# Three branch results summed by accumulating transfers from GpSimd's queue instead of VectorE additions, in a deformable-convolution kernel

## The chip, the cores and the metric

The kernel runs on one core of a Trainium2 chip. The metric is the time of one execution on the device in microseconds, the median over runs. The engines are called as in the profile: PE (TensorE, matmuls), PEld (its weight loads), DVE (VectorE), ACT (ScalarE), POOL (GpSimd) and SP (SyncE, which here only issues transfers). A trailing q, as in SPq, is an engine's own instruction queue.

## The reference, cut to what matters

Two layers act on x of 2 images x 256 channels x 128 x 128 pixels, float32. The change lies in the first one. Three branches with dilations 1, 9 and 12 each sample the image at learned offsets, weigh nine taps, normalise over the channels of each pixel and apply Gelu. Their results and a 1x1 convolution are added; normalisation, a two-layer network per pixel and another normalisation follow.

```python
def _branch(x, w_off, w_def, lw, lb, pad, dil):
    off = _conv(x, w_off, pad, dil)                  # 18 offsets per pixel
    y = _deform_dw(x, off, w_def, pad, dil)          # nine bilinear samples, weighed
    return gelu(_ln2d(y, lw, lb))                    # over the 256 channels of a pixel
...
x1 = _branch(x, off_w1, def_w1, bw1, bb1, 1, 1)
x2 = _branch(x, off_w2, def_w2, bw2, bb2, 9, 9)
x3 = _branch(x, off_w3, def_w3, bw3, bb3, 12, 12)
c = einsum('bchw,oc->bohw', x, conv_w[:, :, 0, 0]) + conv_b
out = _ln2d(x1 + x2 + x3 + c, n1_w, n1_b)
h = gelu(out @ mlp_w1.T + mlp_b1) @ mlp_w2.T + mlp_b2     # per pixel
out = _ln2d(h + out, n2_w, n2_b)
```

In the whole, x + layer0(groupnorm(x)) goes into a second layer of the same form, a 3x3 convolution with ternary weights.

## The kernel before, in words

There are three stages. The first, to about 916 us, takes the group norm's moments, writes a padded pixel-major copy of x to memory (`tables`), computes the offsets, and writes for every branch, tap and row the weights of the bilinear samples (`hats`). The second, the branch stage, runs from 916 to about 5840 us. The third, to the end, is the second layer.

The branch stage (`sample_near`) works in units: image, pair of rows, branch; 2 x 66 x 3 = 396 units. For each unit and each half of the channels, `sample` multiplies eleven tiles `xs` of the table (loaded at L1326) by a matrix `A` (matmul L1468 into `pm`), ACT copies the result to `ev` (L1480), and `accumulate` adds the taps into a ring of rows in SBUF (`ring`, DVE L1429, with a first touch by ACT at L1411). `A` for a unit is the product of the two tiles `hy` and `hx` (DVE L1367), which `load_hats` fetches from `hats` (L1347, three buffers of each) as soon as the product three items earlier has freed one.

Whenever four rows of one branch are finished (a group: 64 groups of 4 rows x 128 pixels over both images), a chain of further steps begins: the generator `PixelTail.branch`. It turns the group to pixel-major form `v` of 128 partitions x 1024 values (transposes L905 and L913, ACT copy L921), takes moments (DVE L1101 to L1106), the power -1/2 on POOL (L1107, L1108), then ACT applies scale, bias and Gelu (`scaled`, L1115). The three branches of a group finish at different times, as their dilations differ, so that the sum goes through memory: branch 0 stores `v` to `g12d` (L1179), branch 1 loads that into the tile `other` (L1186), adds (L1189) and stores the sum (L1191), and branch 2 loads the sum (L1186), adds (L1198) and goes on with it. It loads `xn`, adds the 1x1 convolution (matmul and DVE addition of `product`, L1137 and L1145), normalises, transposes back to `S` (L1154, L1221), computes the network (`hp` L890 into `hT`, `h2` L1137), normalises again and stores `x1d` (L1260).

All engine orders are the program's own: work is recorded in the order in which the Python code runs, and `pin` keeps it. The chains are interleaved with the sampling by hand. `sample` calls `tail.advance()` twice for each unit and half of the channels; each call is one step, in which every chain whose time has come runs to its next `yield`. A `yield` gives up to three values: the steps to wait, the number of buffers that the chain claims from then on, and a flag by which only one flagged chain runs per step. Nine buffers (`VBUFS`) of one rotation hold `v`, `other`, `xn`, `S`, `hT` and `xr`, and `may` lets a chain run only if the claims fit. The set `stored` tells which branch's transfer to `g12d` has been issued; branches 1 and 2 of a group wait for their predecessor there. When sampling is over, the remaining chains run step by step alone; this drain takes from about 5700 to 5840 us.

All plain transfers in this stage are issued by SP, in order. SP stops at a transfer whose source is not ready, and what is behind it stops with it.

Of the kernel before, what the change touches and what calls it, by code (L numbers as in the profile page):

```python
# [14 lines left out]
ALU = mybir.AluOpType  # L15
# [56 lines left out]
def conv_preact_kernel(ctx: ExitStack, tc: tile.TileContext, t: dict, out: bass.AP):  # L72
    nc = tc.nc
# [634 lines left out]
    with ExitStack() as actx:  # L708
        psum = actx.enter_context(tc.tile_pool(name="ps_a", bufs=1, space=PSUM))

        def gps():
# [4 lines left out]
        k = {  # L716
            "dxs": dxs,
            "zero": ap.tile([P, C], F32, name="zero"),
            "wz": ap.tile([P, KC, NZ], F32, name="wz"),
            "shift": ap.tile([P, len(dxs), P], F32, name="shift"),  # L720
            "mid": ap.tile([P, ZG, NOFF], F32, name="mid"),
            "hatw": ap.tile([P, 2, NTAP * NH], BF16, name="hatw"),
            "parts": [ap.tile([P, 2, ZG, P], BF16, name=f"parts{i}") for i in range(3)],
            "zr": ap.tile([P, ZRING, NZ], F32, name="zr"),
# [110 lines left out]
    class Tail:  # L835
# [135 lines left out]
        def branch(self, b, br, g, y):  # L971

            pin = self.pin
            cols = slice(g * NG, (g + 1) * NG)
            gv = g12d[b].rearrange("(k p) f -> p k f", p=P)[:, :, cols]
            z = []
            yield from self.normalised(z, y, (b, br, g))
            v = z[0]
            for c in range(KC):
                pin(  # L980
                    nc.scalar.activation(
                        v[:, c, :], z[1 + c], AF.Gelu,
                        scale=bw[:, br, c : c + 1], bias=bb[:, br, c : c + 1],
                    )
                )
            if br == 0:
                yield 2
                nc.sync.dma_start(gv, v)
                self.stored.add((b, br, g))
                return  # L990
            yield 1, 1 + br
            other = self.tile("other")
            while (b, br - 1, g) not in self.stored:
                yield 1
            nc.sync.dma_start(other, gv)
            if br == 1:
                yield 2
                pin(nc.vector.tensor_tensor(v, v, other, ALU.add))
                yield 2
                nc.sync.dma_start(gv, v)  # L1000
                self.stored.add((b, br, g))
                return
            xn = self.tile("xn")
            nc.sync.dma_start(xn, x[b].rearrange("(k p) h w -> p k (h w)", p=P)[:, :, cols])
            yield 4
            for c in range(KC):
                pin(
                    nc.scalar.activation(
                        xn[:, c, :], xn[:, c, :], AF.Identity, bias=negmean[b][:, c : c + 1]
                    )  # L1010
                )
            yield 1
            yield from self.finish(b, g, v, other, xn)
# [75 lines left out]
    class PixelTail(Tail):  # L1089
# [70 lines left out]
        def branch(self, b, br, g, y):  # L1160

            pin = self.pin
            gv = g12d[b].rearrange("c f -> (c f)").rearrange("(g p e) -> g p e", p=P, e=KC * NG)[g]
            xv = x[b].rearrange("(k p) h w -> p k (h w)", p=P)[:, :, g * NG : (g + 1) * NG]
            yield from self.entered()
            yield 0, 1, True
            v = self.tile("v")
            vf = v.rearrange("p k n -> p (k n)")
            vv = vf.rearrange("p (j c) -> p j c", c=C)
            rows = [vv[:, j, :] for j in range(NG // P)]  # L1170
            self.turned(vv, y, (b, br, g))
            self.read.add((b, br, g))
            rs = self.moments(rows)
            yield 7, min(1 + br, 2), True
            yield from self.scaled(rows, rs, AF.Gelu)
            self.norms -= 1
            if br == 0:
                yield 2
                nc.sync.dma_start(gv, vf)  # L1179
                self.stored.add((b, br, g))  # L1180
                return
            other = self.tile("other")
            of = other.rearrange("p k n -> p (k n)")
            while (b, br - 1, g) not in self.stored:
                yield 1
            nc.sync.dma_start(of, gv)  # L1186
            if br == 1:
                yield 2
                pin(nc.vector.tensor_tensor(vf, vf, of, ALU.add))  # L1189
                yield 2  # L1190
                nc.sync.dma_start(gv, vf)  # L1191
                self.stored.add((b, br, g))
                return
            yield 1, 3
            xn = self.tile("xn")
            nc.sync.dma_start(xn, xv)
            yield 2
            pin(nc.vector.tensor_tensor(vf, vf, of, ALU.add))  # L1198
            yield 2, 2, True
            for c in range(KC):  # L1200
                pin(
                    nc.scalar.activation(  # L1202
                        xn[:, c, :], xn[:, c, :], AF.Identity, bias=negmean[b][:, c : c + 1]
                    )
                )
            yield 1
            pairs = [(xn[:, c, :], convs[b][:, c, :]) for c in range(KC)]
            adds = [self.product("pc1", vv, convb3, pairs, h) for h in range(2)]
            yield 1, 1
            for add in adds:  # L1210
                add()
            yield 2
            yield from self.entered()
            rs = self.moments(rows)
            yield 7, None, True
            yield from self.scaled(rows, rs, AF.Identity)
            self.norms -= 1
            yield 2, 2, True
            S = self.tile("S")
            for c in range(KC):  # L1220
                pin(nc.scalar.copy(S[:, c, :], self.channels(rows, c)))  # L1221
            yield 1, 3
            hT = []
            for m in range(MC):
                if m % KC == 0:
                    hT.append(self.tile("hT"))
                hp = self.bank("hp")
                self.matmul(hp, [(w1[:, c, m * P : (m + 1) * P], S[:, c, :]) for c in range(KC)])
                pin(
                    nc.scalar.activation(  # L1230
                        hT[-1][:, m % KC, :], hp, AF.Gelu, bias=b1[:, m : m + 1]
                    )
                )
                yield 1, 4 if m < MC - 1 else 3
            pairs = [(hT[m // KC][:, m % KC, :], w2[:, m, :]) for m in range(MC)]
            add = self.product("h2", vv, b23, pairs, 0)
            yield 1, 3
            add()
            add = self.product("h2", vv, b23, pairs, 1)
            yield 1, 1  # L1240
            add()
            yield 2, 2
            yield from self.entered()
            rs = self.moments(rows)
            xr = self.tile("xr")
            nc.sync.dma_start(xr, xv)
            yield 7, None, True
            yield from self.scaled(rows, rs, AF.Identity)
            self.norms -= 1
            yield 2  # L1250
            for c in range(KC):
                zc = self.channels(rows, c)
                pin(
                    nc.vector.scalar_tensor_tensor(
                        xr[:, c, :], zc, n2w[:, c : c + 1], xr[:, c, :], ALU.mult, ALU.add
                    )
                )
                pin(nc.vector.bn_stats(stats2[b][:, c, g, :], xr[:, c, :]))
            yield 2, 1
            nc.sync.dma_start(  # L1260
                x1d[b].rearrange("(k p) f -> p k f", p=P)[:, :, g * NG : (g + 1) * NG], xr
            )
# [365 lines left out]
    with cmp.Else():  # L1628
        with ExitStack() as bctx:
            psum = bctx.enter_context(tc.tile_pool(name="ps_b", bufs=1, space=PSUM))  # L1630
            pool = bctx.enter_context(tc.tile_pool(name="bpool", bufs=1))
            k = {
                "A": [pool.tile([PX, 9, RI, WA], F32, name=f"A{i}") for i in range(2)],
            }
# [356 lines left out]
```

## Time and profile before

| | |
|---|---|
| median of 3 runs | 6637.6 us (6625.94 to 6637.77) |
| the profiled execution's own time | 6632.7 us |
| its span | 6630.8 us |
| busy over the span: PE, DVE, ACT, POOL | 95%, 89%, 63%, 10% |
| TensorE clock granted, mean | 0.974 of full speed |
| moved by the DMA engines | 1360 MB, 205 GB/s on average |
| loads `other` (L1186), 512 KB | 128 |
| stores to `g12d` (L1179, L1191), 512 KB | 64 and 64 |
| additions L1189, L1198 | 64 and 64, 1.22 us each |

The profile is of one execution. A group of instructions in it gives line, engine, operation, what is written and read, shape and count, then the busy time in us and the mean of one in ns, then the engine's idle time just before them and what ended most of it. The chain is the sequence of work that ended last, followed back from the last instruction to what released each step. A busy share of PE is not a share of its peak, since matmuls are pipelined and their ends are modelled.

### The profile page before, as it was taken

To read this page: it belongs to the slowest core of one execution; us is meant where nothing else is said; L and a number is where in the kernel's file an instruction comes from. 1 tells how busy PE (TensorE), PEld (TensorE's weight loads), DVE (VectorE), ACT (ScalarE), POOL (GpSimd) and SP (SyncE) were. 2 spreads that over 40 slices of the span, in tenths; PEclk is the share of its full clock that TensorE was granted. 3 is DMA by queue.
4 is the path that set the end of the run, shared out by engine and by line. 5 is a ranking of instruction groups with operands and counts; after the bars stand their busy time and mean duration, and the time that the engine had idled before them with its cause. 6 is when DMAs were issued, how large, how long until landed. Compare 5 with 4: busy or idle time off the path is not lost.

```text
span 6630.8 us, 100591 instructions
## 1 busy us (share of the span) xinstructions
PE 6275.4 (95%) x32242; PEld 4993.0 (75%) x32242; DVE 5906.2 (89%) x13772; ACT 4189.3 (63%) x8690; POOL 686.7 (10%) x665
## 2 busy tenths in 40 slices
PE   6899978999999999999999999999999999989999
PEld 3455558888888888888888888888888888734444
DVE  8766668999999999999778999999999999689996
ACT  2344447777777777777676777777777777554442
POOL 0000000111111111111110111111111111200000
PEclk9999978999999999999999999999999999989999
DMA  8976667877787777787667877788777777343332
GB/s 290 274 214 199 201 169 216 226 217 219 223 225 217 223 217 224 222 222 206 181 194 203 227 219 219 221 223 227 223 217 220 215 222 209 122 164 132 139 139 90
DMA packets 635795, 1360.49 MB, mean 205 GB/s; under 512 B 109592, under 2 KB 290344, under 8 KB 618736
## 3 DMA queue, kind: packets, MB, share of 16 engines
q1 hardware_dynamic: 617328, 1318.97, 68.9%
q10 hardware_dynamic: 17408, 33.56, 1.6%
q8 instruction: 261, 4.28, 0.3%
q14 instruction: 286, 2.34, 0.1%
q0 software_dynamic: 512, 1.34, 0.1%
HBM read 1087.10 MB, written 266.47 MB: 204 GB/s over the span
## 4 chain that ended last, share of the span: by engine, by line
PE 53%; DVE 30%; DMA 8%; ACT 5%; issue 3%; SPq 0%; POOL 0%; DVEq 0%; ACTq 0%; POOLq 0%
PE pm L1468 22%; DVE ring L1429 13%; PE pc L1810 6%; PE hp L890 6%; PE h L1137 5%; DVE A L1367 5%; PE pz L364 4%; DMA hx<-hats 3%; PE pc L1137 3%; DMA xa<-in_x 3%; ACT ev L1480 2%; ACT v L1115 2%; DVE st L1101 1%; PE ph L463 1%; PE tp L905 1%
## 5 line engine op out<-in xcount | busy, mean ns | idle before, releaser
L1468 PE MATMUL pm<-A,xs 96*128 96x216 f32 (+2 forms) x17424 | 3248.5, 343 | 176.4 <-ACT ev L1480 45.4
L1468 PEld LDWEIGHTS pm<-A,xs 96*128 96x128 f32 x17424 | 3049.1, 195 | 374.1 <-ACT ev L1480 119.2
L1429 DVE SCALAR_TENSOR_TENSOR ring<-ev,defw,ring 128x256 f32<-128x256 f32 (+4 forms) x6372 | 2481.2, 451 | 98.1 <-ACT ev L1480 47.8
L1480 ACT COPY ev<-pm 128x432 f32<-128x432 f32 (+4 forms) x4488 | 1987.5, 483 | 869.3 <-PE pm L1468 695.8
L1367 DVE TENSOR_TENSOR A<-hy,hx 96x768 f32<-96x768 f32 (+1 forms) x1124 | 1009.5, 945 | 164.1 <-DMA hx<-hats 89.8
L1107 POOL TENSOR_TENSOR rs<-rs,mhalf 128x4 f32<-128x4 f32 x320 | 472.0, 1475 | 4202.5 <-DVE rs L1106 3543.9
L1810 PE MATMUL pc<-cring,signs 128*128 128x512 bf16 x3456 | 757.9, 382 | 17.0 <-ACT cring L1727 7.4
L1115 ACT ACTIVATE v<-v,rs 128x256 f32<-128x256 f32 x1280 | 694.4, 594 | 16.7 <-POOL rs L1108 16.6
L1810 PEld LDWEIGHTS <-signs 128*128 128x128 bf16 x3456 | 339.6, 98 | 434.6 <-issue 27.7
L890 PE MATMUL hp<-S,w 128*128 128x512 f32 x1024 | 493.9, 607 | 0.8 <-ACT S L1221 0.8
L364 PE MATMUL pz<-wz,xa 128*128 128x486 f32 x1024 | 461.6, 578 | 25.3 <-DVE zr L371 25.3
L1137 PE MATMUL h<-w,hT 128*128 128x256 f32 x2048 | 477.1, 379 | 0.0
L1101 DVE BATCH_NORM_STATS2 st<-v 128x6 f32<-128x256 f32 x1280 | 446.9, 410 | 30.8 <-ACT v L921 30.8
L1411 ACT ACTIVATE ring<-ev,defw 128x256 f32<-128x256 f32 (+1 forms) x856 | 404.5, 485 | 24.2
L1137 PEld LDWEIGHTS h<-w,hT 128*128 128x128 f32 x2048 | 369.3, 190 | 65.5 <-issue 1.0
L364 PEld LDWEIGHTS pz<-wz,xa 128*128 128x128 f32 x1024 | 189.2, 191 | 189.3 <-issue 126.1
L921 ACT COPY v<-tp 128x512 f32<-128x512 f32 x384 | 207.8, 598 | 182.7 <-PE tp L913 182.4
L1230 ACT ACTIVATE hT<-hp,b 128x512 f32<-128x512 f32 x256 | 176.1, 688 | 218.6 <-PE hp L890 214.6
L890 PEld LDWEIGHTS hp<-S,w 128*128 128x128 f32 x1024 | 196.7, 197 | 139.4 <-issue 121.3
L470 ACT ACTIVATE hb<-ph 96x512 f32<-96x512 f32 (+1 forms) x384 | 209.8, 596 | 144.2 <-PE ph L463 135.6
L1137 PE MATMUL pc<-convw,xn 128*128 128x256 f32 x1024 | 271.1, 393 | 2.4 <-ACT xn L1202 2.4
L371 ACT COPY zr<-pz 128x486 f32<-128x486 f32 x128 | 72.1, 564 | 256.5 <-PE pz L364 253.8
(246 smaller groups left out, 5132.5 us busy)
## 6 DMA issues: line engine op xcount, KB each, us to landing
hy<-hats SPq DMA_DIRECT2D x1112, 288.0 KB
hx<-hats SPq DMA_DIRECT2D x1112, 288.0 KB
xs<-tables SPq DMA_DIRECT2D x1452, 96.0 KB
g12d<-v SPq DMA_DIRECT2D x128, 512.0 KB
other<-g12d SPq DMA_DIRECT2D x128, 512.0 KB
hats<-hb SPq DMA_DIRECT2D x64, 720.0 KB
hats<-hb SPq DMA_DIRECT2D x64, 576.0 KB
xa<-in_x ACTq DMA_DIRECT2D x64, 512.0 KB
```

The source lines that it names most:

```text
L364: nc.tensor.matmul(pz[:, 0:NZ], lhsT=xt[:, c, r, :], rhs=k["wz"][:, c, :], start=c == 0, stop=c == KC - 1,)
L890: nc.tensor.matmul(out, lhsT=w, rhs=v, start=i == 0, stop=i == n - 1)
L1101: pin(nc.vector.bn_stats(st[:, j, :], rows[j]))
L1107: nc.gpsimd.tensor_tensor(rs[:, 0, :], rs[:, 0, :], mhalf[:, 0:n], ALU.pow)
L1115: nc.scalar.activation(row, row, func, scale=rs[:, 0, j : j + 1], bias=rs[:, 1, j : j + 1])
L1137: nc.tensor.matmul(bank[:, j, :], lhsT=v[:, px], rhs=w, start=False, stop=i == len(pairs) - 1,)
L1367: nc.vector.tensor_tensor(dst, hy[:, i0:i1].rearrange("p i t w -> p t i w"), hx[:, i0:i1].rearrange("p i t w -> p t i w"), ALU.mult,)
L1411: pin(nc.scalar.mul(dst, src, w))
L1429: pin(nc.vector.scalar_tensor_tensor(dst, src, w, dst, ALU.mult, ALU.add))
L1468: nc.tensor.matmul(pv[:, j, :, m0:m1, :], lhsT=xts[b, Rt][t][:, c * P : (c + 1) * P], rhs=A[:, y0:y1, m0:m1, AO + t * CI : AO + (t + 1) * CI],
L1480: nc.scalar.copy(dst.rearrange("p m (t j) -> p t m j", j=CI), pm[:, 0 : len(ts), 0:n].rearrange("p t (m j) -> p t m j", j=CI),)
L1810: nc.tensor.matmul(pc, lhsT=signs[:, k, (h * 3 + t) * 3 + kx, m * P : (m + 1) * P], rhs=xc[:, i, k, t * JC : (t + 1) * JC, kx : kx + W], s ...
```

## The change

Branch 1 no longer loads `other`, adds and stores: GpSimd issues one transfer that adds `v` onto the values in `g12d`. Branch 2 no longer loads and adds either: GpSimd issues one transfer that adds the values in `g12d` onto `v` in SBUF. The tile `other` is gone, and with it 128 loads and 64 stores of SP and 128 additions of DVE. Branch 1 and branch 2 claim one buffer instead of two while they wait for the moments. Branch 1 marks its result as stored four steps earlier. Branch 2 waits the same number of steps up to its next ACT work, one and four instead of one, two and two, and claims two buffers instead of three meanwhile.

```diff
@@ PixelTail.branch
             rs = self.moments(rows)
-            yield 7, min(1 + br, 2), True
+            yield 7, 1, True
             yield from self.scaled(rows, rs, AF.Gelu)
...
-            other = self.tile("other")
-            of = other.rearrange("p k n -> p (k n)")
             while (b, br - 1, g) not in self.stored:
                 yield 1
-            nc.sync.dma_start(of, gv)
             if br == 1:
-                yield 2
-                pin(nc.vector.tensor_tensor(vf, vf, of, ALU.add))
-                yield 2
-                nc.sync.dma_start(gv, vf)
+                nc.gpsimd.dma_start(gv, vf, accum_op=ALU.add)
                 self.stored.add((b, br, g))
                 return
-            yield 1, 3
+            nc.gpsimd.dma_start(vf, gv, accum_op=ALU.add)
+            yield 1, 2
             xn = self.tile("xn")
             nc.sync.dma_start(xn, xv)
-            yield 2
-            pin(nc.vector.tensor_tensor(vf, vf, of, ALU.add))
-            yield 2, 2, True
+            yield 4, 2, True
```

In the changed kernel the accumulating transfer of branch 1 stands at L1185, that of branch 2 at L1188; the lines up to L1179 keep their numbers, and those after the edit are seven lower (L1326, L1347, L1367, L1429, L1468 and L1480 become L1319, L1340, L1360, L1422, L1461 and L1473).

## The prediction

> **What bounds the kernel now.** I read the span by stages first. The branches run from about 916 to 5700 us; before them lies the offset stage, after them a drain to 5840 and the second layer, neither of which the change touches except the drain. The table of busy time by stage:
>
> ```profile
> core 0: us, PE busy (x) PEld busy (x) DVE busy (x) ACT busy (x) POOL busy (x), PEclk, DMA share, GB/s
> 916.00:5700.00 4784.00, 4614.24 (x24864) 4115.21 (x24865) 4451.39 (x11227) 3415.48 (x7664) 656.98 (x620) 0.98 0.77 216
> 5700.00:5840.00 140.00, 115.26 (x501) 78.92 (x500) 71.35 (x243) 64.99 (x122) 22.52 (x33) 0.90 0.29 101
> ```
>
> PE is busy 96%, DVE 93%, the DMA engines 77%, POOL 14%. PE leaves 4784 - 4614 = 170 us idle: no relief of another engine can give more in this stage, unless PE's long matmul records hide gaps (matmul ends are modelled, so some do). Two engines are nearly full, so I read the groups for what the additions cost, then the chain for how many of them lie on the path.
>
> ```profile
> L1189 DVE TENSOR_TENSOR v<-v,other 128x1024 f32<-128x1024 f32 x64 | 77.9, 1218 | 2.0 <-DMA other<-g12d 1.9 <-issue 0.2
> ...
> L1198 DVE TENSOR_TENSOR v<-v,other 128x1024 f32<-128x1024 f32 x64 | 77.7, 1214 | 0.0
> ```
>
> The two additions take 1.22 us each, and cost DVE 1.13 us from one start to the next. DVE waits for their operand 1.9 us in all: the loads are well hidden. The chain that ended last, 2215 to 2240 us (start, duration, what):
>
> ```profile
> 2214.99 2.29 DVE ring L1429 x6
> 2217.28 1.13 DVE v L1198
> 2218.42 0.41 DVE ring L1429
> 2218.82 0.14 SPq L1347
> 2218.96 0.05 issue
> 2219.01 5.46 DMA hx<-hats
> ...
> 2235.49 0.11 DVE v L1189
> 2235.60 0.09 issue
> 2235.68 0.02 DVEq L1367
> 2235.70 0.91 issue
> 2236.61 2.69 DVE A L1367 x3
> ```
>
> Both additions are on it here. The second is cut into four pieces because the chain steps to the semaphore instruction behind it, but 2235.49 to 2236.61 is all DVE inside that addition. Read in this way, 100 us at a time, the chain holds 42 of the 128 additions, 45 us together. Elsewhere the path is in PE (L1468, L890, L1137), and an addition there is cover. The path also enters hats loads, 5.46 us here.
>
> The SP queue's waits from 1300 to 5600 us (total us, times, longest):
>
> ```profile
> SPq L1347 <- DVE A L1367: 771.5, 463, 15.3
> SPq L1326 <- PE pm L1468: 680.2, 894, 14.3
> SPq L1191 <- DVE v L1189: 345.8, 54, 8.1
> SPq L1179 <- ACT v L1115: 245.7, 52, 8.4
> SPq L1347 <- DVE ring L1429: 208.3, 452, 2.1
> SPq L1186 <- PE h L1137: 140.3, 27, 6.9
> ```
>
> SP stands for 486 us (L1191, L1186) on the very steps that the change takes from it, in front of the hats loads. But most of the time the load behind would have waited for L1367 anyway.
>
> **What the Trainium skill says.** "DMA: Bandwidth & Descriptors", section on SWDGE, HWDGE and iDMA: an accumulating transfer must be issued by GpSimd, whose cores write its descriptors; the same page, "Issuing engines are not separate DMA queues": all queues end in the same 16 engines. "Collectives: The Full Stack", section on the bandwidth ceiling: an add inside a transfer is not slow by its arithmetic but by its two source reads, and ran at about half the rate of a copy. "SBUF — State Buffer", "Who interferes with whom": DVE instructions with two SBUF inputs contend with GpSimd instructions that read SBUF. The trace of before has no accumulating transfer, so it can't confirm the second and third; it agrees that POOL is uneven (L1107, the same 128x4 power, takes 1006 to 2548 ns).
>
> **The change part by part.**
>
> *DVE loses 128 additions.* On the path 45 us go. Of the other 86 (97 us) some would surface once the path moves; I take a tenth, -10. Bounds of the two together: -26 if PE takes over wherever it was just behind (26 is about what remains if only the pieces named as additions count), -100 if DVE's slack of 7% is what makes PE wait.
>
> *SP loses 128 loads of `other` (median 527 ns to issue) and 64 stores (326 ns)*: 67 + 21 = 88 us of issuing, and the 486 us of standing. SP's own pieces in the chain from 1300 to 5600 us sum to only 11 us, so I take -5; bounds 0 and -25. SP still stands at L1179.
>
> *POOL gains 128 transfers to issue.* The nearest row is the gather of 128 rows, L565, 987 ns each: 126 us on an engine with 4127 us free. Each waits in POOL's own order, for ACT's last Gelu of that `v` and, in branch 2, for the landing of branch 1's accumulation. What is queued behind is the next power L1107 and product L1108, which ACT needs in L1115. Who waits for that now:
>
> ```profile
> L1108 POOL TENSOR_TENSOR rs<-rs x320: 198/409/4867, 1040.5 to 5825.7; 128x4 f32<-128x4 f32 x160
> ...
> who waited for it (us, times):
>   ACT v L1115: 16.6, 3
> ```
>
> Three waits in 320, because the code puts 7 steps between them. A step is 4784 us / (396 units x 2 halves x 2) = 3.0 us, so some 20 us are allowed. An issue of 1 us and a few us of waiting for ACT fit: 0. Bounds 0 and +40. The wait for branch 1's landing is also covered in the steady part: in the built order its accumulation stands 88 calls of L1468 ahead, at 66 calls per 37 us some 49 us.
>
> *The data in flight.* Branch 2's accumulation into `v` has 1 + 4 + 1 + 1 = 7 steps, 21 us, before L1145 adds into the same `v`; if it lands later, DVE stops in order and everything behind with it. At the page's fit for GpSimd's path ("Anatomy of one DMA", 2 us + bytes / 436 GB/s) twice 512 KB takes 4.4 us, an estimate; the crowded hats loads show 5.5 us for 288 KB. I expect 5 to 10 us. Covered.
>
> *The DMA engines.* Per group of four rows before: one store, load, store, load = 4 copies. After: one store and two accumulations at two copies each = 5. A copy of 512 KB takes 216 GB/s / 0.77 = 281 GB/s, 1.9 us of all engines. So 64 x 1.9 = 120 us more on 77%, two and a half points. Loads make up some 6% of the chain from 1300 to 5600 (252 us: hx 172, xs 53, hy 27), so +7; bounds -10 (accumulation as cheap as a copy) and +120.
>
> *Buffers.* `other` leaves the rotation of 9, and the hold at the 7-step wait falls from 2 to 1. In the built order the stores of x1d move by a few L1468 calls only (the last inside the loop from the 8702nd to the 8698th), and both programs have 340 calls of tail matmuls after the last L1468. So the schedule stays: 0, bounds -10 and +10.
>
> *The drain, 5700 to 5840.* Here steps pass without sampling between them, so cover is thin: POOL meets L1185 and L1188 close together, waiting for landings with powers behind. Four groups finish here. I take +8, bounds -8 (seven additions gone) and +25.
>
> Sum: -45 - 10 - 5 + 7 + 8 = -45 us against the profiled execution's 6632.7, which gives 6588. The median of the runs, 6637.6, lies 4.9 above that execution, inside the runs' own spread of 12. I put the same 4.9 on top: **6593**.
>
> **The rivals.**
>
> *Accumulating transfers clog the DMA engines: slower.* If each costs three copies or more, a group takes 1 + 3 + 3 = 7 copies, DMA share rises by 64 x 3 x 1.9 / 4784 = 8 points, and hats or xs loads behind one are 3.8 us later (two extra copies). Today some 46 loads (252 / 5.5) are on the path for some 350 units, 13%; at one in five late loads on the path, 128 x 3.8 x 0.2 = +97, less the 45 + 10 + 5 of gains, plus 8: 6685. It decides from about 2.2 us of extra engine time per accumulation (128 x 2.2 x 0.2 = 56). For it: hats loads on the chain already, DMA 77% busy. Against: the page's halved rate, not a third, and the freed SP queue.
>
> *POOL stands, and the powers come late: slower or even.* The point is a stand over some 12 us less the issue. At +40 the sum is about even, 6633. Against it: POOL is 86% idle, and in steady state what its transfers wait for is long past.
>
> *PE binds at once: no change.* PE's waits there name ACT's copies of `ev`, 54.6 us, and of `S`, 41.5; only part of the first goes back to DVE. Then 45 shrinks to 15 or 20, and drain and DMA give it back: 6630. Against: the many stretches like the quoted one, in which DVE and a load alternate.
>
> *That the additions are not really replaced*: the built order has 128 accumulating transfers on POOL and no addition on DVE. Out.
>
> **How the numbers follow.** A measurement tells about 0.2%, 13 us, from no change. Forecast 0.70, its own range 6540 to 6624, all faster; PE binds 0.08, within 0.2%; DMA engines 0.17 and POOL 0.05, slower. The range takes the large end of DVE's gain (-100 with SP's -15: 6525) and the DMA rival's value: 6525 to 6688, leaving out the worst of that rival and little below.
>
> **What would show it.** Right: DVE's busy time falls by some 150 us with L1189 and L1198 gone; PE's idle time in the branch stage falls from 170 us toward 125; SP's waits at L1191 and L1186 vanish; ACT still hardly waits for L1108; L1145 does not wait for the new transfers. Wrong: DVE's wait for hx (89.8 us over the stage now) doubling, a DMA share at 85% or more, L1145 or L1108 appearing as long waits, the drain growing by over 25 us.

## The result, and the profile after

The changed kernel takes 6615.5 us (median of 12 runs) against 6636.9 before (12 runs). The ratio is 0.9968, with a 95% interval of 0.9957 to 0.9978: 21 us faster, 15 to 29. Forecast were 45: the direction is right, the size is not. The profiled execution took 6623.9 us (span 6622.0), near the upper end of the runs (6600.6 to 6627.6), so its trace is read for causes and the runs for sizes.

The changed kernel's busy time by stage, to be held against the prediction's first table:

```profile
core 0: us, PE busy (x) PEld busy (x) DVE busy (x) ACT busy (x) POOL busy (x), PEclk, DMA share, GB/s
916.00:5700.00 4784.00, 4617.54 (x24891) 4117.20 (x24892) 4327.25 (x11125) 3415.70 (x7675) 770.18 (x743) 0.98 0.78 209
5700.00:5840.00 140.00, 109.05 (x478) 74.83 (x477) 65.88 (x232) 65.85 (x118) 25.39 (x38) 0.89 0.41 120
```

In the branch stage DVE does 124 us less, and PE 3 us more. DVE was relieved as planned; PE got nearly nothing of it in this execution. So the question is what DVE does with the time. Its waits from 1300 to 5600 us (us in total, times, longest), the kernel before:

```profile
DVE A L1367 <- PE pm L1468: 66.7, 51, 4.6
DVE ring L1429 <- ACT ev L1480: 43.8, 48, 2.8
DVE A L1367 <- DMA hx<-hats: 43.5, 38, 6.1
```

and the changed one:

```profile
DVE A L1360 <- PE pm L1461: 120.3, 62, 7.3
DVE A L1360 <- DMA hx<-hats: 90.1, 89, 3.7
DVE ring L1422 <- ACT ev L1473: 49.5, 50, 3.6
```

Two waits have about doubled. The first is good news: DVE is now ahead and waits until PE has read the old `A`. The second is a loss: 89 times instead of 38, DVE stands for the weights `hx`, which are late. (Over the whole stage, 916 to 5700 us, it goes from the 89.8 us of the prediction to 133.7: not doubled, but of the signs of being wrong that the prediction named it is the one that moved.)

On SP the waits for the two steps are gone, and the same time stands at others (changed kernel, 1300 to 5600 us):

```profile
SPq L1340 <- DVE A L1360: 1017.9, 454, 15.5
SPq L1319 <- PE pm L1461: 534.7, 850, 10.1
SPq L1179 <- ACT v L1115: 403.4, 52, 11.0
SPq L1253 <- DVE xr L1247: 299.0, 51, 7.9
```

The 486 us at L1191 and L1186 are gone. Instead SP stands 246 us more at the hats loads (772 to 1018), which wait for a free buffer, 191 more at the store of `x1d` (108 to 299) and 158 more at L1179, and 145 less at the `xs` loads. Here the queue mostly changed the place where it stands.

### The profile page after: what moved, and what is told of

Its sections match the earlier page's. It is cut to its first block, busy times and chain, and to the rows that moved or that the text cites. A ratio compares the mean times of both kernels' runs of the same rounds, so it can differ in the third digit from the quotient of the medians.

```text
span 6622.0 us, 100200 instructions
## 1 busy us (share of the span) xinstructions
PE 6280.3 (95%) x32242; PEld 4993.8 (75%) x32242; DVE 5768.3 (87%) x13644; ACT 4184.2 (63%) x8690; POOL 801.1 (12%) x793
## 5 line engine op out<-in xcount | busy, mean ns | idle before, releaser
L1461 PE MATMUL pm<-A,xs 96*128 96x216 f32 (+2 forms) x17424 | 3238.6, 342 | 168.9 <-ACT S L1214 45.1
L1461 PEld LDWEIGHTS pm<-A,xs 96*128 96x128 f32 x17424 | 3045.8, 194 | 363.2 <-ACT ev L1473 110.3
L1422 DVE SCALAR_TENSOR_TENSOR ring<-ev,defw,ring 128x256 f32<-128x256 f32 (+4 forms) x6372 | 2478.9, 451 | 90.5 <-ACT ev L1473 52.9
L1473 ACT COPY ev<-pm 128x432 f32<-128x432 f32 (+4 forms) x4488 | 1983.1, 483 | 880.7 <-PE pm L1461 684.0
L1360 DVE TENSOR_TENSOR A<-hy,hx 96x768 f32<-96x768 f32 (+1 forms) x1124 | 1014.8, 946 | 278.5 <-DMA hx<-hats 133.7
L1107 POOL TENSOR_TENSOR rs<-rs,mhalf 128x4 f32<-128x4 f32 x320 | 477.0, 1491 | 3402.8 <-DVE rs L1106 3364.1
L1115 ACT ACTIVATE v<-v,rs 128x256 f32<-128x256 f32 x1280 | 694.2, 594 | 24.2 <-POOL rs L1108 24.2
L1404 ACT ACTIVATE ring<-ev,defw 128x256 f32<-128x256 f32 (+1 forms) x856 | 404.5, 485 | 24.2
L463 PE MATMUL ph<-planes,hatw 128*96 128x512 bf16 (+3 forms) x768 | 219.9, 400 | 20.9 <-DVE planes L453 10.8
```

The lines of the kernel that those rows point to most:

```text
L1107: nc.gpsimd.tensor_tensor(rs[:, 0, :], rs[:, 0, :], mhalf[:, 0:n], ALU.pow)
L1115: nc.scalar.activation(row, row, func, scale=rs[:, 0, j : j + 1], bias=rs[:, 1, j : j + 1])
L1360: nc.vector.tensor_tensor(dst, hy[:, i0:i1].rearrange("p i t w -> p t i w"), hx[:, i0:i1].rearrange("p i t w -> p t i w"), ALU.mult,)
L1404: pin(nc.scalar.mul(dst, src, w))
L1422: pin(nc.vector.scalar_tensor_tensor(dst, src, w, dst, ALU.mult, ALU.add))
L1461: nc.tensor.matmul(pv[:, j, :, m0:m1, :], lhsT=xts[b, Rt][t][:, c * P : (c + 1) * P], rhs=A[:, y0:y1, m0:m1, AO + t * CI : AO + (t + 1) * CI],
```

## The experiments

Each kernel was timed against the kernel before on the same chip, and its ratio is to that. The series ran on different chips, so ratios are compared and not times. One thousandth is 6.6 us.

| kernel | ratio | 95% interval | us to before |
|---|---|---|---|
| changed | 0.9968 | 0.9957 to 0.9978 | -21 |
| no_adds | 0.9910 | 0.9892 to 0.9927 | -60 |
| no_sum | 0.9910 | 0.9893 to 0.9927 | -60 |
| plain_copies | 0.9914 | 0.9896 to 0.9932 | -57 |
| old_claims | 0.9977 | 0.9966 to 0.9988 | -15 |
| acc_b1 | 0.9962 | 0.9949 to 0.9976 | -25 |
| acc_b2 | 0.9937 | 0.9920 to 0.9953 | -42 |
| hats3_v8 | 1.0002 | 0.9993 to 1.0011 | +1 |
| hats4 | 0.9903 | 0.9884 to 0.9921 | -64 |
| hats3_v9 | 0.9999 | 0.9990 to 1.0008 | -1 |
| hats4_v9 | 0.9871 | 0.9856 to 0.9886 | -86 |
| before_hats4_v9 | 0.9962 | 0.9948 to 0.9975 | -25 |
| plain_hats4_v9 | 0.9862 | 0.9847 to 0.9877 | -92 |

The us column is the ratio's distance from one, times 6637. A difference of two rows carries the noise of both: 0.0054 between the changed kernel and plain_copies is 36 us, give or take 14.

One thing runs beside all these ratios. The mean granted TensorE clock was 0.972 for the kernel before (its 65 runs in the three series of experiments), 0.974 for the changed kernel, 0.976 for plain_copies and 0.978 for hats4_v9. Among those 65 runs a clock higher by 0.001 goes with 3.9 us less. By that slope, an estimate, about a quarter of the larger gains goes with the clock. Whether the clock is a cause or follows from what the engines do isn't separated here; the order of the kernels named stays the same.

### What are the additions worth, and what do the transfers cost?

Two theories stood against each other. *Cover*: an addition is worth half of what the chain shows, because PE or a load takes over at once. *Given back*: the additions are worth all of it, and the transfers that replace them cost half.

**no_adds** is the kernel before without its additions:

```diff
-                yield 2
-                pin(nc.vector.tensor_tensor(vf, vf, of, ALU.add))
-                yield 2
+                yield 4
...
-            yield 2
-            pin(nc.vector.tensor_tensor(vf, vf, of, ALU.add))
-            yield 2, 2, True
+            yield 4, 2, True
```

> The kernel before without its 128 additions (it leaves the sum of the branches out; loads of other, stores and steps stay). Theory 'cover' (PE and the hats loads take over as soon as an addition is gone, and the accumulating transfers cost little): about the changed kernel's gain, 6637 - 20 = 6617. Theory 'given back' (the additions are worth the 45 us that the chain shows, and the transfers cost half of it): 6637 - 45 = 6592 or less.

Measured: 0.9910, 60 us (48 to 72) faster. *Cover* falls: the additions are worth the 45 us that the chain held, or more.

**no_sum** is the changed kernel without its transfers:

```diff
-                nc.gpsimd.dma_start(gv, vf, accum_op=ALU.add)
...
-            nc.gpsimd.dma_start(vf, gv, accum_op=ALU.add)
```

> The changed kernel without its two accumulating transfers (it leaves the sum of the branches out): the most that any cheap way of adding could give. 'Cover': 6615 less a few us for three of five 512 KB transfers per group less, 6605 to 6612. 'Given back': 6615 - 30 = 6585 or less.

Measured: 0.9910, the same as no_adds. So the 192 plain transfers that no_adds still has on SP's queue cost nothing that can be told (to within some 16 us), although they keep the DMA engines busy: over all queues 4725 us of the 16 engines' time in no_adds, 4434 in no_sum. The most to be had from this change was some 60 us. The changed kernel gets 21 of them.

**plain_copies** has the transfers on POOL, but as plain copies:

```diff
-                nc.gpsimd.dma_start(gv, vf, accum_op=ALU.add)
+                nc.gpsimd.dma_start(gv, vf)
...
-            nc.gpsimd.dma_start(vf, gv, accum_op=ALU.add)
+            nc.gpsimd.dma_start(vf, gv)
```

> The changed kernel with plain copies in the place of the accumulating ones, same queue and waits (it leaves the sum out). It tells the adding inside the transfer from its issue and waits on POOL. 'Cover': 6615, no change from the changed kernel. 'Given back' by the DMA engines: some 10 to 20 us faster than the changed kernel, 6600; 'given back' by POOL's issue and waits: 6615.

Measured: 0.9914. Waits and order on POOL cost nothing that can be told. It is the adding inside the transfer that takes 0.9968 - 0.9914 = 0.0054, 36 us: more than the 10 to 20 that I expected. The issue is shorter with plain copies too, a median of 0.62 us against 0.93; that this isn't what costs is seen only further on, where the two kernels with a fourth buffer come out level. The DMA queues of plain_copies, q0 being POOL's (packets, MB, share of 16 engines over the span):

```profile
q1 hardware_dynamic: 589680, 1218.29, 64.9%
q0 software_dynamic: 18944, 68.46, 2.9%
```

and those of the changed kernel:

```profile
q1 hardware_dynamic: 589680, 1218.29, 64.0%
q0 software_dynamic: 18944, 68.46, 5.6%
```

Packets and bytes are the same; the time is double, 371 us (5.6% of 6622.0) against 191 (2.9% of 6588.1), or, over all packets of q0, 313 ns of an engine for a packet against 161. The landing tells it as well. POOL's transfers of the changed kernel, branch 2's at L1188:

```profile
L1188 POOL DMA_DIRECT2D v<-g12d x64: 872/925/946, 1235.0 to 5743.1; - x64
...
DMA to landing us min/median/max: 5.1/9.5/10.6
```

This last line tells only 16 of the 64 landings, and late ones: plain copies on the same semaphore land after a median of 8.2 us, all 64 plain ones after 5.5. Taken for all 64 from the semaphores' updates (the last one before that semaphore's next transfer is issued), the medians are 8.1 us against 5.5 for branch 2 and 7.1 against 5.1 for branch 1.

**old_claims** gives the changed kernel the buffer claims of before, and issues branch 1's transfer four steps later:

```diff
-            yield 7, 1, True
+            yield 7, min(1 + br, 2), True
...
+                yield 4
                 nc.gpsimd.dma_start(gv, vf, accum_op=ALU.add)
...
-            yield 1, 2
+            yield 1, 3
```

> The changed kernel with the buffer claims and the store's step of before: branch 1 claims two buffers and issues four steps later. If the new interleaving of the chains eats gain or makes it, this moves by 10 us or more from 6615; my prediction had it at 0, so 6615 within 5.

Measured: 0.9977, 6 us behind the changed kernel with intervals that overlap. The new claims are worth nothing or a little.

### Through what do 36 us get lost?

The suspect is the hats load. In the trace of the changed kernel I took each of DVE's waits for `hx` in 1300 to 5600 us and asked whether the awaited load, from issue to landing, was in flight together with one of POOL's transfers (landings taken as above). 80 of 96 waits of 50 ns and over, 77 of 91 us, had such company; of all `hx` loads of that stretch 38% had (390 of 1015). With plain copies it is 23 of 64 waits, 20 of 40 us.

The loads themselves are later too. From issue to landing, so without what SP stood before the issue, the median `hx` load takes 5.5 to 5.6 us in the kernel before, the changed one, plain_copies and no_sum alike. But the slowest tenth takes 8.4 us or more in the changed kernel, against 6.9 before, 7.3 with plain copies and 6.7 in no_sum. Whether this lateness is what costs the time, the next experiments try.

**acc_b1** and **acc_b2** leave one of the two transfers accumulating:

```diff
 # acc_b1
-            nc.gpsimd.dma_start(vf, gv, accum_op=ALU.add)
+            nc.gpsimd.dma_start(vf, gv)
 # acc_b2
-                nc.gpsimd.dma_start(gv, vf, accum_op=ALU.add)
+                nc.gpsimd.dma_start(gv, vf)
```

> The changed kernel with branch 1 accumulating in memory and branch 2 only loading (it leaves branch 2's own values out of the sum). If every accumulating transfer costs the same on the DMA engines, it lies half-way between plain copies (6591) and the changed kernel (6615): 6603. If accumulating in memory is the dear one: 6612; if it is the one into SBUF: 6593.

> The changed kernel with branch 1 storing plainly and branch 2 accumulating into SBUF (it leaves branch 0 out of the sum). Same cost for both: 6603; SBUF the dear one, or branch 2's landing too late for L1145: 6612; memory the dear one: 6593.

Measured: 0.9962 and 0.9937. Branch 1's transfer into memory takes 0.0048 from plain copies, as much as both together; branch 2's into SBUF takes 0.0023, with intervals that overlap plain copies' (0.9920 to 0.9953 against 0.9896 to 0.9932). DVE's hx waits from 1300 to 5600 us go the same way, here in plain_copies, acc_b1 and acc_b2:

```profile
DVE A L1360 <- DMA hx<-hats: 39.9, 57, 3.6
DVE A L1360 <- DMA hx<-hats: 103.1, 90, 4.4
DVE A L1360 <- DMA hx<-hats: 50.5, 62, 3.4
```

On the engines the two differ less: q0 is at 4.5% and 4.1%, so 1.6 and 1.2 points above plain copies. Engine time alone doesn't give the difference; that it depends on which load a transfer meets is a reading. Whether branch 1's is dearer because it writes to memory or because of the moment at which it is issued isn't separated here.

**hats4** gives hy and hx a fourth buffer, so that a late load has one more item's time to arrive. **hats3_v8** is its control, with the same room made for it:

```diff
-VBUFS = 9
+VBUFS = 8
...
-        part = pool.tile([P, 3, C], BF16, name="part")
+        part = pool.tile([P, 3, C], BF16, name="part", tag="v", bufs=VBUFS)
 # hats4 alone; hx likewise
-                hy = pool.tile([PX, RI, 3, W], F32, name="hy", tag="hy", bufs=3)
+                hy = pool.tile([PX, RI, 3, W], F32, name="hy", tag="hy", bufs=4)
...
-                    load_hats(items.index((u, ky)) + 3)
+                    load_hats(items.index((u, ky)) + 4)
...
         load_hats(2)
+        load_hats(3)
```

> The changed kernel with four buffers of hy and of hx instead of three, loads issued four items ahead; to make room the rotation of v holds 8 buffers instead of 9 and one small early tile lies in it. If hats loads that come late behind accumulating transfers are what gives the gain back, DVE's waits for hx (90 us from 1300 to 5600 us) fall under 30 and the time goes to about 6590, level with plain copies, and clearly under hats3_v8. If they are not the cause (the waits only stand where PE would have stood anyway): like hats3_v8.

> The control of hats4: the changed kernel with 8 buffers in the rotation of v and still three of hy and hx. The change took other out of the rotation, so 8 should do: 6615 within 8 us; if chains now wait for buffers, over 6625.

Measured: 0.9903 against 1.0002 for the control. The control is the miss here: eight buffers in the rotation, or what else made the room, cost the changed kernel all of its gain. The fourth hats buffer brings 0.0099, 66 us, and DVE's waits for `hx` nearly vanish, from the first line (hats3_v8) to the second (hats4):

```profile
DVE A L1360 <- DMA hx<-hats: 93.2, 86, 6.6
DVE A L1360 <- DMA hx<-hats: 9.1, 11, 3.4
```

**hats4_v9**, **hats3_v9**, **before_hats4_v9** and **plain_hats4_v9** make the room in another way and keep nine buffers. The three with hats4 in the name add the fourth buffers as above; they start from the changed kernel, the kernel before, and plain_copies:

```diff
-    reach = const.tile([P, 2, NB * H], F32, name="reach")
+        early = actx.enter_context(tc.tile_pool(name="early", bufs=1))
+        reach = early.tile([P, 2, NB * H], F32, name="reach")
...
-                xt = pool.tile([PX, C], F32, name="xs", tag="xs", bufs=18)
+                xt = pool.tile([PX, C], F32, name="xs", tag="xs", bufs=17)
...
-        part = pool.tile([P, 3, C], BF16, name="part")
+        part = pool.tile([P, 3, C], BF16, name="part", tag="v", bufs=VBUFS)
```

> The changed kernel with a fourth buffer of hy and hx and the full rotation of nine; room comes from freeing reach after the first stage, the small early tile in the rotation, and 17 instead of 18 xs tiles. hats3_v8 lost some 30 us by its eight buffers, so with nine: 6575 - 25 = 6550, the best version so far. If the eight buffers cost nothing once hats loads are early: 6575.

> The control: the changed kernel with the same room made, but three buffers of hy and hx. If 17 xs tiles and the moved tiles are harmless: 6615 to 6620, as the changed kernel.

> The kernel before with the same fourth buffers. If the wait for hats is mainly a product of the accumulating transfers, it gains less than the changed kernel does from them: about 20 us, to 6620 (its hx waits of 43 us from 1300 to 5600 us are half on the path). If the fourth buffer is worth 60 us to any version, hats loads bounded all of them: 6580.

> hats4_v9 with plain copies in the place of the accumulating ones (it leaves the sum out). If the accumulations cost time only by making hats loads late, nothing is left of their 36 us: equal to hats4_v9 within 8 us. If they also act in another way (POOL's order, late landing, memory), it stays 20 us or more faster.

The room itself is again not free: hats3_v9 is at 0.9999, 0.0031 behind the changed kernel, against my expectation. Which of its three moves costs that wasn't tried. DVE's waits in it, from 1300 to 5600 us:

```profile
DVE A L1361 <- DMA hx<-hats: 117.2, 99, 3.9
DVE A L1361 <- PE pm L1462: 112.6, 58, 7.3
```

and in hats4_v9:

```profile
DVE A L1361 <- PE pm L1462: 132.4, 63, 7.3
...
DVE A L1361 <- DMA hx<-hats: 18.4, 16, 6.0
```

The wait for hats goes from 117 to 18 us, and the time from 0.9999 to 0.9871, or 6551 us on the scale of 6637, as expected. The accumulating transfers are still as dear on the engines (q0 at 5.8%), and the slowest tenth of the `hx` loads is as late as ever (8.6 us or more). But with a buffer more this costs nothing that can be told: hats4_v9 and plain_hats4_v9 lie at 0.9871 and 0.9862, 6 us apart, give or take 14. In plain_hats4_v9 DVE's wait is:

```profile
DVE A L1361 <- DMA hx<-hats: 9.7, 5, 5.8
```

As far as can be told the 36 us are gone, though some 20 could be left. That shows the path: an accumulating transfer makes a hats load late, and the late load stops DVE. A plain-copies kernel with the same room but three buffers was not run, so the price of the accumulation in just that room isn't known.

The fourth buffer does more than take this price away. plain_copies, which accumulates nothing, gains 0.0052 by it (0.9914 to 0.9862), 35 us. So late hats loads seem to cost time without any accumulation, too.

The kernel before gains 0.0038 from the same fourth buffers, 25 us where I expected about 20, and the changed one 0.0097 against 0.9968; the room's cost is in both. The two changes help each other. A reading that fits, though no run isolates it: before, DVE was mostly late itself where the hats loads came just in time.

hats4_v9, at 6559 us (6647 before, in the same series), beats both kernels, by 1.3% the one before and by 1.0% the changed one.

## Why the prediction was right or wrong

The time lies inside the forecast's own range (6540 to 6624), but the gain is 21 us where 45 were forecast. Put together from the experiments it is 60 (the additions) - 36 (the adding inside the transfers) = 24, with SP and POOL at nothing.

**The additions: right, a little low.** Forecast were 55 us (45 on the chain and a tenth of the rest), measured 60. The way of counting, with the pieces behind L1189 taken as part of the addition, fits this better: the pieces that bear its name alone gave 26, below the interval's low end of 48. Which additions on the chain were worth what, no run tells.

**SP: right in kind.** -5 was put down, and no_sum against no_adds shows no difference. That the load behind would have waited anyway fits SP's waits above.

**POOL: right.** Issue was put at 0.99 us and takes 0.93. ACT waited for L1108 16.6 us before and 24.2 now, in five waits. plain_copies shows that the waits cost nothing, and hats4_v9 beside plain_hats4_v9 that the issue doesn't either. The contention that the prediction listed for POOL played no part that can be seen: with 128 additions gone from DVE, the power L1107 takes a mean of 1491 ns against 1475.

**The landing: right.** 5 to 10 us were expected, the medians are 7.1 (branch 1) and 8.1 (branch 2); the estimate of 4.4 us was too low. L1145 does not appear as waiting for them.

**The DMA engines: this is the step that failed.** The Trainium skill's "Collectives: The Full Stack", section on the bandwidth ceiling, says that a step that adds ran at about half the rate of one that copies, for its two source reads. Here, on quite another path, q0's 371 against 191 us agree with the half; the reason no run here shows. The prediction took that price, but turned it into time wrongly. It took 120 us of extra engine time, the fifth copy per group, and charged the 6% of it that loads hold of the chain: +7. Measured are 36, give or take 14. A mean share does not say what a transfer costs that arrives beside a load with no slack. The engines' total rose by only 31 us (4707 to 4738 over all queues), since q1 fell by 330 us as q0 rose by 366, and the stage's DMA share only moved from 0.77 to 0.78. And the 291 us of engine time by which no_adds and no_sum differ cost nothing that can be told. It was not the amount of load but the lateness of single loads.

The rival "accumulating transfers clog the DMA engines" named this path. What it had wrong was the price (3.8 us for each, where it is (371 - 191) / 128 = 1.4) and so the sign; its point of decision, 2.2 us, was not reached. (Its sum gives 6683, not 6685.) Its rule, one in five of the extra time, happens to hit: 180 us times 0.2 is 36. The one in five was a guess, and acc_b1 and acc_b2, with 1.6 and 1.2 points of extra engine time for some 32 and 15 us, don't follow it, so this is luck rather than a rule to carry. With the forecast's own price it would have missed the other way: 128 x 1.9 x 0.2 = 49 leaves almost no gain.

**The drain: cautious.** +8 were put down. From the last sampling matmul (5700.3 and 5692.5 us) to the last moments of `xr` (5831.5 and 5822.6) it takes 131.2 us before and 130.1 after.

**Buffers and claims: right**, within old_claims' interval.

**PE binds at once: refuted** by no_adds' 60 us, though PE's idle time in the table falls only from 170 to 166 us in the profiled execution. That PE's long records hide gaps, as the prediction named for a possibility, fits this; it was not measured.

## What to carry to other kernels

Ask of a transfer that is put beside others not only how much time it takes of the engines, but which load with no slack it will meet: DMA engines that were busy 78% of the time here still delivered single loads late, and an engine that follows in order then stands. When a relieved engine shows a new wait for loads, give that load one more buffer before judging the change: here the change alone brought 0.3%, together with a fourth buffer 1.3%. Read a chain by adding the unnamed pieces behind an instruction to it; here they were 19 us beside 26.

## What was not expected of the hardware

An accumulating transfer of 512 KB from GpSimd's queue costs more than a plain one in every respect seen here: twice the engine time (313 against 161 ns for a packet), and about half as much again to land (7.1 and 8.1 against 5.1 and 5.5 us) and to issue (0.93 against 0.62 us). The one into memory seems to cost the kernel more than the one into SBUF (0.0048 and 0.0023, each give or take some 0.0023), with 1.6 and 1.2 points of q0 above plain copies; why is open.
